# The last chunk's edge sums kept on chip and spread by a 0/1 product

## The chip, the cores and the metric

The kernel is one program on one core of a Trainium2 chip. The core has TensorE (PE; its weight loads are listed as PEld), VectorE (DVE), ScalarE (ACT), GpSimd (POOL) and SyncE (SP), each with its own queue of instructions, which it takes strictly in order. DMAs are issued by the SP, ACT and POOL queues. The metric is the device time of one execution in microseconds, as a median of several runs; lower is better.

## The reference

One graph layer over 10,000 nodes of 512 features, 160,000 edges sorted by `dst`, all in float32:

```python
xn = _layernorm(x, axis=-1)
x = x + gnn(xn) + attention(xn)        # gnn: relu(segment_sum(h[src'] * w, dst') + bias), h = xn @ W
x = x + experts(_layernorm(x, axis=-1))
```

`gnn` is called with the arrays `src` and `dst`. For each edge it takes a row of normalised features, times the edge's weight, summed into the node of the other end; since the product with `W` is linear, the kernel sums rows first and multiplies by `W` (`wg`) afterwards. `attention` is linear attention with softmax over the features of the queries and over the tokens of the keys, followed by a layer norm without mean shift; `experts` weighs six two-layer networks by a router that sees the mean over all tokens, so it can't be finished before the last row of `x` is known.

## The kernel before

The nodes are cut into 20 chunks (`NCH`): 19 of 512 rows (128 partitions x `SUB` = 4) and a last one of 272 (68 partitions x 4). There are three stages.

**Keys and queries** (up to 1350 us) makes keys, queries and the attention's matrix `G`. From its third chunk on, edges run beside it.

**Rows** (to 2143 us) goes through the chunks. `attention(c)` multiplies the stored queries of chunk c with `mix` (`po`, L1048) and normalises; it runs `MIXED` = 3 chunks ahead. The loop of L1063 then takes the chunk's edge sums `at` (fetched by `gathered`), transposes them into `aT` (`nodes_rows`, L1071, ACT copies them out of PSUM), multiplies by `wg` (`pg`, L1087), adds bias, relu and attention on DVE, stores the row to `x1_d` (L1091) and takes statistics.

**Experts** (from 2143 us) goes through the chunks again: rows come back from `x1_d` (`rows_in`, four DMAs), ACT normalises them (`normalising`, L351), DVE transposes them and makes sums of halves (`turned_in`, `xs`), and PE multiplies by weights and sums of weights (`w_sum`, made by `sums_of_weights` once `w1` is loaded).

**The edges.** The 1250 tiles of 128 edges are cut into 866 windows of at most two tiles; four windows make one of 217 groups (`NQ`). For a group, POOL gathers the source rows by an indirect DMA a tile (`msg`, L583), DVE makes the selecting matrix `sel` (L589, L591), PE sums them into a 128 x 512 PSUM tile `pm` (L601: 32 rows a window), ACT copies it to `part` (L604) and stores it in `part_d` (L605). There are 24 `msg` buffers, three `part` buffers and two for `pm`. `work(us)` (L698) sets the pace: every product that is put out lets `done[1]` grow by an assumed cost, 0.83 us a matmul, and as many groups as fit are put out with it. `far_enough(c)` (L996) forces all groups out that chunk c's sums need, before they are fetched.

Two neighbouring windows can share nodes, so each window's first four rows hold what belongs to the window before. `carry(w, end)` (L672) is a DMA on POOL's queue that adds such rows in DRAM, over the ranges between the entries of `CARRIES`; the fetch `gathered(c)` (L1013) is an indirect DMA on POOL's queue that reads by the rows of `row_of`, which `find_rows` works out.

The end of the rows stage: in the turn of chunk 17 (`NCH - 3`), `all_edges_in` (L1005) puts out all groups still missing (211 to 216), the last carry and the fetches of chunks 18 and 19, frees the edge buffers (`edge_ctx.close()`) and asks for the expert weights, which take their place. Only then come chunk 19's attention, chunk 17's transposes and its product. In the turn of chunk 18 the first expert rows are asked for (L1117).

**Order.** Inside `manual_schedule` PE runs its instructions in the order in which the program writes them. On the other engines, and on the DMA queues, a planner orders the instructions by its own cost model and by the order of writing, and adds the semaphores. `behind(inst, other)` makes one instruction follow another on its engine. A buffer of a pool is reused once its readers and DMAs are done, a freed pool's memory likewise.

If the input doesn't fit the windows' assumptions, which DVE counts into `n_odd`, `general_path` does all edges again by scatter; on the given input it isn't taken.

Of the kernel before, what the change touches and what calls it, by code (L numbers as in the profile page):

```python
# [9 lines left out]
F32 = mybir.dt.float32  # L10
# [7 lines left out]
P = 128  # L18
SQ = 32
# [18 lines left out]
MIXED = 3  # L38

AT_HAND = [(5, 320), (7, 384), (8, 424), (9, 472), (10, 520), (11, 560), (12, 604), (13, 640), (14, 680), (15, 716), (16, 752),  # L40
           (17, 788), (18, 820)]
# [11 lines left out]
]  # L53


@with_exitstack
def gps_layer_kernel(
# [91 lines left out]
    ZERO_ROW = NQ * P  # L149
# [74 lines left out]
    def sums_of(o, a11, a12, a21, a22):  # L224

        nc.vector.tensor_tensor(o[0], a21, a22, ALU.add)  # L226
        nc.vector.tensor_tensor(o[2], a11, a21, ALU.subtract)  # L227
        nc.vector.tensor_tensor(o[1], o[0], a11, ALU.subtract)  # L228
        nc.vector.tensor_tensor(o[3], a12, o[1], ALU.subtract)
# [149 lines left out]
    def sums_of_weights():  # L379
        w1_sb, w1_sum = held_w["w1"], held_w["w1_sum"]  # L380
        p_half, q_half = slice(0, PAIRS * P), slice(PAIRS * P, 2 * PAIRS * P)
        sums_of([w1_sum[:, i] for i in range(4)], w1_sb[:, :KH, p_half], w1_sb[:, KH:, p_half],
                w1_sb[:, :KH, q_half], w1_sb[:, KH:, q_half])
# [4 lines left out]
    with ExitStack() as ph:  # L388
# [54 lines left out]
        n_odd = ep.tile([1, 1], I32, name="n_odd")  # L443

# [79 lines left out]
        def window_at(node, more):  # L524
            tile_no = NET * (node / N) ** 0.5 + more
            return min(max(int(tile_no / 2 if tile_no < 2 * PAIRED else tile_no - PAIRED), 0), NW)

        def span(c):
            return window_at(chunks[c][0], -SPARE), window_at(chunks[c][0] + SUB * chunks[c][1], SPARE)

        def spans_hold():
            for c, (b, r) in enumerate(chunks):
                for i, w, op, edge in ((0, span(c)[0], ALU.is_le, b), (1, span(c)[1], ALU.is_ge, b + SUB * r)):
                    at = 3 + len(AT_HAND) + 2 * c + i
                    nc.vector.tensor_scalar(count[:, at : at + 1], bases[:, w : w + 1], float(edge // SUB), None, op0=op)
# [59 lines left out]
        def edges_summed(i, batch, m, sel):  # L595

            pm = psum_e.tile([P, D], F32, name="pm")
            for j in range(batch):
                for h in range(GROUP):
                    k = h * batch + j  # L600
                    nc.tensor.matmul(pm[h * WIN : (h + 1) * WIN, :], sel[:, k, :], m[k] if k < len(m) else m[0],  # L601
                                     start=j == 0, stop=j == batch - 1, skip_group_check=True)
            part = pools["w"].tile([P, D], F32, name="part")
            nc.scalar.copy(part, pm)  # L604
            nc.scalar.dma_start(part_d[i * P : (i + 1) * P, :], part)  # L605
# [39 lines left out]

        def next_nodes():
            pn = psum.tile([P, 1], F32, name="pnext", tag="ps")
            nc.tensor.transpose(pn[:CHAINED], bases[0:1, 1 : CHAINED + 1], ident[0:1, 0:1])
            nc.vector.tensor_copy(nexts[:CHAINED], pn[:CHAINED])
# [26 lines left out]
        carried = []  # L676
        for i in range(PARTS):
            carried.append((past(CHAINED // GROUP, i * LAG), partial(carry_loads, i)))
            carried.append((past(CHAINED // GROUP, (i + 1) * LAG), partial(carry_chained, i)))
# [5 lines left out]
        ahead = [AHEAD]  # L685
        EARLY_TOTAL = PRODUCT * KB * ROWS_IN * 3 * KB
# [11 lines left out]
        def work(us):  # L698

            done[1] += us  # L700
            if not pools:

                normal_rows(int(done[1] / EARLY_TOTAL * (NCH + 1)) + 4 - len(normal))
                return
            edges_to(groups_of(int(done[1] / pace[0])))
# [14 lines left out]
        def all_edges(fp):  # L720
# [12 lines left out]
            nc.vector.tensor_copy(row_of, four)  # L733
            dst_sb = fp.tile([P, NET], I32, name="dst_far")
# [121 lines left out]
        for c, (_, r) in enumerate(chunks):  # L856
# [67 lines left out]
            if c == CHECKED:  # L924
                next_nodes()
                oddities()
            if c >= CHECKED:
                find_rows(c, added)
                if c < 2 * CHECKED:
                    find_rows(c - CHECKED, added)  # L930
# [65 lines left out]
        def far_enough(c):  # L996

            for n, w in AT_HAND:
                if c < n:
                    edges_to(min(NQ, past(w // GROUP, lag_of(w) + LEAD) + 1))  # L1000
                    return w * WIN
            assert not pools
            return ZERO_ROW + P

        def all_edges_in():  # L1005
            edges_to(NQ)
            carry(CARRIES[-1], NW - 1)
            assert not carried
            pools.clear()
            edge_ctx.close()  # L1010
            experts_weights()

        def gathered(c):  # L1013
            r = chunks[c][1]
            n_rows = far_enough(c)
            at = io.tile([P, SUB, D], F32, name="at", tag="at" if c < NCH - 1 else "qT")
            nc.gpsimd.indirect_dma_start(
                out=at[:r].rearrange("p s d -> p (s d)"), out_offset=None, in_=by_four[: n_rows // SUB, :],
                in_offset=bass.IndirectOffsetOnAxis(ap=row_of[:r, c : c + 1], axis=0))
            return at  # L1020
# [17 lines left out]
        def attention(c, beside):  # L1038
# [3 lines left out]
            qT, xt = held.pop("last") if c == NCH - 1 else (queries_in(c), rows_again(c))  # L1042
# [20 lines left out]
        for c, (_, r) in enumerate(chunks):  # L1063
            ot, at = mixed.pop(0), ats.pop(0)
            aT = io.tile([P, KB, SUB * P], F32, name="aT", bufs=1)

            if c == NCH - 3:
                all_edges_in()
                ats += [gathered(c + 1), gathered(c + 2)]
# [4 lines left out]
            if c + MIXED < NCH - 1:  # L1074
                mixed.append(attention(c + MIXED, nodes_rows))
            elif c == NCH - 3:
                mixed.append(attention(NCH - 1, nodes_rows))
            else:
                nodes_rows()
            if c < NCH - 3:  # L1080
                ats.append(gathered(c + 1))
            if c == NCH - 4:
                held["last"] = queries_in(NCH - 1), rows_again(NCH - 1)

            for s in range(SUB):
# [3 lines left out]
                nc.vector.tensor_tensor(po[:r, :], po[:r, :], bias_b[:r], ALU.add)  # L1089
# [17 lines left out]
            if c == NCH - 3:  # L1107
                sums_of_weights()
            if c == NCH - 2:
                io_f["in"] = ctx.enter_context(tc.tile_pool(name="f_in", bufs=1, reuse_waits="tile"))  # L1110

                io_f["squares"] = io_f["in"].tile([P, P // SQ, P], F32, name="squares")
                for b in range(P // SQ):
                    nc.vector.tensor_copy(
                        io_f["squares"][:, b].rearrange("k (g t) -> k g t", t=SQ),
                        ident[:, None, b * SQ : (b + 1) * SQ].to_broadcast([P, P // SQ, SQ]))
                xn = rows_in(0)  # L1117
                st = small.tile([P, P // SQ, 1, SUB, 2], F32, name="st_sq", bufs=1)
                stats_of_squares(st, 0)
                for step in normalising(0, xn, st[:, :, 0]):  # L1120
                    step()
                turn = turned_in(0, rows_turned(0, xn))
# [350 lines left out]
```

## Time and profile before

| | |
|---|---|
| median of 3 runs | 3536.73 us (3527.2 to 3548.53) |
| profiled execution | 3518.48 us, its span 3516.7 us |
| PE busy | 3256.7 us (93%), 12819 matmul instructions |
| DVE, ACT, POOL busy | 1766.5, 831.1, 1311.2 us |
| mean granted clock of TensorE | 0.961 |
| edge gathers (`msg`) | 1250 issues, 984 ns each on POOL |
| last edge gather issued / last group's matmuls | 2059.89 us / 2067.9 us |
| first expert matmul | 2142.57 us |

The profile is of one execution. Times in it count from the first instruction. A line of the timeline gives start, length, engine, source line, operation, what it writes and reads, and in brackets how long the engine was idle before and what ended that wait ("issue": nothing that the profile shows). A float32 matmul appears as two records; 0.43 us apart for 512 columns. A table of windows gives the busy time of each engine in a stretch, the granted clock, and the share of time that the DMA engines were busy.

### The profile page before, as it was taken

How to read it: one execution, taken by the hardware profiler on the slowest of the kernel's cores; microseconds unless marked ns; L12 is line 12 of the kernel's file. 1: busy time of each engine (PE TensorE's matmuls, PEld its weight loads, DVE VectorE, ACT ScalarE, POOL GpSimd, SP SyncE). 2: the span in 40 equal slices, each digit the busy share in tenths (PEclk: the TensorE clock that was granted, in tenths of full speed). 3: DMA queues.
4: the chain of work that ended last, by engine and by line, in shares of the span. 5: the costliest groups of instructions: out<-in, count | busy, mean ns of one | idle time of the engine just before them, and what ended most of it. 6: DMA issues, size and time to landing. Idle time of an engine off the chain costs nothing. (4 is left out here: it accounts for less than half of the span.)

```text
span 3516.7 us, 36142 instructions
## 1 busy us (share of the span) xinstructions
PE 3256.7 (93%) x12819; PEld 1916.0 (54%) x12819; DVE 1766.5 (50%) x3902; ACT 831.1 (24%) x1674; POOL 1311.2 (37%) x1421
## 2 busy tenths in 40 slices
PE   6899998988999989898998988999999999999998
PEld 3433333333333333333333335888888888888886
DVE  6644445444444425564565557445445544544542
ACT  5321212121112112121222113222222222222221
POOL 3466666665666656676676630000000000000000
PEclk8999999999999979899999988999999999999999
DMA  9677777776777878898998882221212212122111
GB/s 392 235 217 249 227 247 248 254 223 208 227 223 243 247 275 318 313 332 293 318 336 301 294 268 61 60 75 58 60 57 76 60 49 84 49 60 73 60 37 38
DMA packets 216735, 654.39 MB, mean 186 GB/s; under 512 B 34425, under 2 KB 74361, under 8 KB 188831
## 3 DMA queue, kind: packets, MB, share of 16 engines
q0 software_dynamic: 104096, 354.29, 32.0%
q1 hardware_dynamic: 69992, 175.33, 15.2%
q10 hardware_dynamic: 42452, 122.31, 9.0%
q8 instruction: 105, 1.72, 0.2%
q14 instruction: 90, 0.74, 0.1%
HBM read 491.21 MB, written 166.63 MB: 187 GB/s over the span
## 5 line engine op out<-in xcount | busy, mean ns | idle before, releaser
L583 POOL DMA_INDIRECT msg<-xn_d,src_sb x1250 | 1229.9, 984 | 634.4 <-issue 287.2
L601 PE MATMUL pm<-msg,sel 128*32 128x512 f32 x2504 | 351.7, 617 | 54.5 <-issue 44.5
L911 PE MATMUL pc<-xn,ek 128*128 128x512 f32 (+1 forms) x640 | 306.5, 624 | 20.5 <-issue 15.0
L209 PE MATMUL po<-G,qT 128*128 128x512 f32 (+1 forms) x640 | 302.0, 613 | 13.0 <-issue 12.2
L209 PE MATMUL pg<-wq,aT 128*128 128x512 f32 (+1 forms) x640 | 301.3, 617 | 10.2 <-issue 9.0
L604 ACT COPY part<-pm 128x512 f32<-128x512 f32 x217 | 127.1, 586 | 733.9 <-PE pm L601 276.0
L601 PEld LDWEIGHTS pm<-msg,sel 128*32 128x32 f32 x2504 | 66.1, 110 | 302.7 <-issue 266.2
L209 PEld LDWEIGHTS pg<-wq,aT 128*128 128x128 f32 (+1 forms) x640 | 117.7, 192 | 195.7 <-issue 184.7
L911 PEld LDWEIGHTS pc<-xn,ek 128*128 128x128 f32 (+1 forms) x640 | 122.7, 199 | 177.4 <-issue 164.7
L209 PEld LDWEIGHTS po<-G,qT 128*128 128x128 f32 (+1 forms) x640 | 117.4, 191 | 185.6 <-issue 181.4
L243 PE MATMUL px<-xnT,w_sb 128*128 128x256 f32 (+1 forms) x800 | 204.6, 379 | 6.8 <-DVE u L1290 6.8
L243 PE MATMUL p<-kq_sum,xs_b 128*128 128x512 f32 (+1 forms) x432 | 201.4, 600 | 3.2 <-issue 2.4
L166 DVE BATCH_NORM_STATS2 st<-ot 128x6 f32<-128x512 f32 (+1 forms) x160 | 110.3, 689 | 178.5 <-issue 119.2
L243 PE MATMUL px<-w_sb,hh 128*128 128x256 f32 (+1 forms) x800 | 185.7, 379 | 0.0
L243 PE MATMUL py<-xs,w_sum 128*128 128x256 f32 (+1 forms) x800 | 185.3, 374 | 0.0
L243 PE MATMUL p<-wk,xnT 128*128 128x512 f32 (+1 forms) x288 | 148.1, 637 | 34.9 <-issue 26.7
L243 PE MATMUL py<-w_sum,hh 128*128 128x256 f32 (+1 forms) x800 | 179.2, 379 | 0.0
L589 DVE TENSOR_TENSOR sel<-iota_w,place 128x128 f32<-128x128 f32 (+2 forms) x217 | 74.5, 344 | 206.1 <-remote 86.2
L243 PEld LDWEIGHTS px<-xnT,w_sb 128*128 128x128 f32 x800 | 150.7, 192 | 29.9 <-DVE u L1290 10.0
L243 PEld LDWEIGHTS py<-w_sum,hh 128*128 128x128 f32 (+1 forms) x800 | 150.0, 188 | 22.7
L243 PEld LDWEIGHTS px<-w_sb,hh 128*128 128x128 f32 (+1 forms) x800 | 150.0, 188 | 22.7
L243 PEld LDWEIGHTS py<-xs,w_sum 128*128 128x128 f32 x800 | 149.8, 190 | 19.9
(298 smaller groups left out, 4577.4 us busy)
## 6 DMA issues: line engine op xcount, KB each, us to landing
part_d<-part ACTq DMA_DIRECT2D x217, 256.0 KB
msg<-xn_d,src_sb POOLq DMA_INDIRECT x1250
xn<-in_x SPq DMA_DIRECT2D x19, 1024.0 KB
xn_d<-xn ACTq DMA_DIRECT2D x19, 1024.0 KB
qT_d<-qT ACTq DMA_DIRECT2D x19, 1024.0 KB
qT<-qT_d SPq DMA_DIRECT2D x19, 1024.0 KB
xt<-in_x SPq DMA_DIRECT2D x19, 1024.0 KB
x_d<-ot SPq DMA_DIRECT2D x19, 1024.0 KB
```

The lines of the kernel that those rows point to most:

```text
L166: nc.vector.bn_stats(st[:r, s, :], t[:r, s, :])
L209: nc.tensor.matmul(po[:r, :], t[:, kb, s * r : (s + 1) * r], w[:, kb, :], start=kb == 0, stop=kb == KB - 1)
L243: nc.tensor.matmul(o, lhs[j], rhs[j], start=start and j == 0, stop=stop and j == n - 1, skip_group_check=True)
L583: nc.gpsimd.indirect_dma_start(out=m[k], out_offset=None, in_=xn_d, in_offset=bass.IndirectOffsetOnAxis(ap=src_sb[:, t0 + k : t0 + k + 1], ...
L589: nc.vector.tensor_tensor(sel[:, :n], iota_w[:, None, :].to_broadcast([P, n, WIN]), place[:, t0 : t0 + n, None].to_broadcast([P, n, WIN]), ...
L601: nc.tensor.matmul(pm[h * WIN : (h + 1) * WIN, :], sel[:, k, :], m[k] if k < len(m) else m[0], start=j == 0, stop=j == batch - 1, skip_gro ...
L604: nc.scalar.copy(part, pm)
L911: nc.tensor.matmul(pc, ek[:r, s, cb * P : (cb + 1) * P], xn[:r, s, :], start=s == 0, stop=s == SUB - 1)
```

## The change

The edge sums of the last six groups (211 to 216, `ON_CHIP` = 211) stay in SBUF, in two tiles of three groups (`parts`, in the buffers of the queries `qT`). Only groups up to 213 (`STORED` = 214) are also written to DRAM. A carry is made up to window 853 instead of 820 for chunk 18; there is none behind it.

The last chunk's sums are made on PE. `nodes_on_chip` (in chunk 5 of the keys stage) notes for each row of a kept group which node it stands for. `numbered` compares these with the numbers of the last chunk's 272 nodes: a 0/1 matrix of 128 x 272 for each of the six groups. `last_sums` multiplies the kept sums with it, 128 features at a time, giving the transposed sums that the product with `wg` wants, the carry's addition included. It is called twice: with the first four groups (`FIRST_SUMS`) after chunk 17's product, written to `aT_last` by ACT copies, and with the other two in the turn of chunk 19, together with `at` (by a product with the identity), added on DVE. On the given input `at` is now a fetch of 68 rows that are all the row of zeros (`row_of` = `ZERO_ROW`), so that the general path can still use it.

The order changes too. Chunk 19's attention is written in the turn of chunk 16. Chunk 17's transposes and product come before `all_edges_in`, with the groups held back at 215 (`limit`) until then. The first expert rows are asked for ahead of the expert weights. The sums of weights move behind the first expert inputs, and chunk 19's additions are ordered behind them.

```diff
+FIRST_SUMS = 4
 AT_HAND = [(5, 320), ..., (16, 752),
-           (17, 788), (18, 820)]
+           (17, 788), (18, 820), (19, 853)]
...
-    ZERO_ROW = NQ * P
+    ON_CHIP = window_at(N, NET, chunks[-1][0], -3) // GROUP
+    STORED = -(-CARRIES[-1] // GROUP)
+    ZERO_ROW = STORED * P
...
-            part = pools["w"].tile([P, D], F32, name="part")
+            if i < ON_CHIP:
+                part = pools["w"].tile([P, D], F32, name="part")
+            else:
+                if (i - ON_CHIP) % 3 == 0:
+                    parts.append(io.tile([P, 3, D], F32, name="parts", tag="qT"))
+                part = parts[-1][:, (i - ON_CHIP) % 3, :]
             nc.scalar.copy(part, pm)
-            nc.scalar.dma_start(part_d[i * P : (i + 1) * P, :], part)
+            if i < STORED:
+                nc.scalar.dma_start(part_d[i * P : (i + 1) * P, :], part)
...
+        def nodes_on_chip():
+            nc.vector.memset(node_of, FAR)
+            for h in range(GROUP):
+                n = -(-(NW - ON_CHIP * GROUP - h) // GROUP)
+                for q, next_one in ((WIN, 0), (SUB, 1)):
+                    rows = slice(h * WIN, h * WIN + q)
+                    at = node_of[rows, :n]
+                    w = ON_CHIP * GROUP + h + next_one
+                    nc.vector.tensor_scalar(at, bases[rows, w : w + GROUP * (n - 1) + 1 : GROUP], float(SUB), spare[rows],
+                                            op0=ALU.mult, op1=ALU.add)
+                    nc.vector.tensor_scalar(at, at, float(-N - h * WIN - (0 if next_one else SUB)), None, op0=ALU.add)
+            nc.vector.tensor_scalar(row_of[:, NCH - 1 :], four[:, NCH - 1 :], 0.0, float(ZERO_ROW // SUB),
+                                    op0=ALU.mult, op1=ALU.add)
...
-            edges_to(groups_of(int(done[1] / pace[0])))
+            edges_to(min(groups_of(int(done[1] / pace[0])), limit[0]))
...
             if c == CHECKED:
+                nodes_on_chip()
                 next_nodes()
                 oddities()
             if c >= CHECKED:
-                find_rows(c, added)
+                if c < NCH - 1:
+                    find_rows(c, added)
...
         def all_edges_in():
             edges_to(NQ)
-            carry(CARRIES[-1], NW - 1)
+            ats.append(gathered(NCH - 2))
+            ats.append(gathered(NCH - 1))
             assert not carried
             pools.clear()
             edge_ctx.close()
+            io_f["in"] = ctx.enter_context(tc.tile_pool(name="f_in", bufs=1, reuse_waits="tile"))
+            rows_first = rows_in(0)
             experts_weights()
+            io_f["squares"] = ...
+            return rows_first
+
+        def numbered():
+            b, r = chunks[-1]
+            mine = io.tile([P, NQ - ON_CHIP + 1, SUB, r], F32, name="mine", tag="xt", bufs=1)
+            number = mine[:, NQ - ON_CHIP]
+            nc.gpsimd.iota(number, pattern=[[1, SUB], [SUB, r]], base=b, channel_multiplier=0,
+                           allow_small_or_imprecise_dtypes=True)
+            for g in range(NQ - ON_CHIP):
+                nc.vector.tensor_scalar(mine[:, g], number, node_of[:, g : g + 1], None, op0=ALU.is_equal)
+            return mine
+
+        def last_sums(o, mine, groups, at):
+            n = SUB * chunks[-1][1]
+            for kb in range(KB):
+                kbs = slice(kb * P, (kb + 1) * P)
+                pt = psum.tile([P, SUB * P], F32, name="pt", tag="ps")[:, :n]
+                for g in groups:
+                    nc.tensor.matmul(pt, parts[g // 3][:, g % 3, kbs], mine[:, g].rearrange("p s n -> p (s n)"),
+                                     start=g == groups[0], stop=at is None and g == groups[-1], skip_group_check=True)
+                if at is None:
+                    nc.scalar.copy(o[:, kb, :n], pt)
+                    continue
+                r = chunks[-1][1]
+                for s in range(SUB):
+                    nc.tensor.matmul(pt[:, s * r : (s + 1) * r], at[:r, s, kbs], ident[:r, :r],
+                                     start=False, stop=s == SUB - 1, skip_group_check=True)
+                nc.vector.tensor_tensor(o[:, kb, :n], o[:, kb, :n], pt, ALU.add)
...
-            aT = io.tile([P, KB, SUB * P], F32, name="aT", bufs=1)
-
-            if c == NCH - 3:
-                all_edges_in()
-                ats += [gathered(c + 1), gathered(c + 2)]
+            aT = io.tile([P, KB, SUB * P], F32, name="aT", bufs=1) if c < NCH - 1 else aT_last
...
-            if c + MIXED < NCH - 1:
+            if c + MIXED < NCH:
                 mixed.append(attention(c + MIXED, nodes_rows))
-            elif c == NCH - 3:
-                mixed.append(attention(NCH - 1, nodes_rows))
+            elif c < NCH - 1:
+                nodes_rows()
             else:
-                nodes_rows()
+                last_sums(aT, mine, range(FIRST_SUMS, NQ - ON_CHIP), at)
...
+            if c == NCH - 3:
+                limit[0] = ON_CHIP + FIRST_SUMS
             for s in range(SUB):
...
-                nc.vector.tensor_tensor(po[:r, :], po[:r, :], bias_b[:r], ALU.add)
+                added = nc.vector.tensor_tensor(po[:r, :], po[:r, :], bias_b[:r], ALU.add)
+                if c == NCH - 1:
+                    behind(added, weights_summed)
...
             if c == NCH - 3:
-                sums_of_weights()
+                mine = numbered()
+                aT_last = io.tile([P, KB, SUB * P], F32, name="aT_last", tag="ot", bufs=MIXED + 2)
+                edges_to(limit[0])
+                last_sums(aT_last, mine, range(FIRST_SUMS), None)
+                rows_first = all_edges_in()
             if c == NCH - 2:
-                io_f["in"] = ...
-                xn = rows_in(0)
                 st = small.tile([P, P // SQ, 1, SUB, 2], F32, name="st_sq", bufs=1)
                 stats_of_squares(st, 0)
-                for step in normalising(0, xn, st[:, :, 0]):
+                for step in normalising(0, rows_first, st[:, :, 0]):
                     step()
-                turn = turned_in(0, rows_turned(0, xn))
+                turn = turned_in(0, rows_turned(0, rows_first))
+                weights_summed = sums_of_weights()
```

## The prediction

> **What bounds the kernel now.** I read the table of windows first, because the edit touches one place: the end of the edge sums and the start of the expert stage. Columns: window, its length, busy us (instructions) of PE, PEld, DVE, ACT, POOL, then granted clock, DMA share, GB/s.
>
> ```profile
> 1450.00:2020.00 570.00, 531.61 (x1830) 199.72 (x1828) 323.82 (x840) 116.52 (x225) 390.59 (x392) 0.96 0.90 314
> 2020.00:2070.00 50.00, 34.03 (x141) 11.55 (x141) 25.66 (x70) 9.09 (x19) 27.73 (x29) 0.80 0.86 289
> 2070.00:2143.00 73.00, 59.32 (x182) 26.22 (x181) 55.52 (x112) 15.43 (x38) 6.33 (x45) 0.92 0.68 188
> ...
> 2197.00:3517.00 1320.00, 1301.49 (x5940) 1109.36 (x5939) 626.66 (x1256) 335.17 (x812) 0.00 (x0) 0.99 0.20 60
> ```
>
> PE is the bound before 2020 and after 2197. Between them, in 123 us, it idles 30 us and runs at a lowered clock. So whatever moves the start of the experts (2142.57) moves the end one for one. PE's timeline shows where the idle time lies (start, length, instruction group, idle time before it):
>
> ```profile
> 2029.07 1.49 PE L601 MATMUL pm<-msg,sel 128*32 128x512 f32 x8 [2.47 <-ACT part L604]
> 2033.89 1.93 PE L601 MATMUL pm<-msg,sel 128*32 128x512 f32 x8 [3.32 <-issue]
> ...
> 2057.26 1.93 PE L601 MATMUL pm<-msg,sel 128*32 128x512 f32 x8 [3.65 <-issue]
> 2064.32 4.15 PE L601 MATMUL pm<-msg,sel 128*32 128x512 f32 x24 [5.12 <-ACT part L604]
> 2068.40 10.52 PE L209 MATMUL po<-G,qT 128*68 128x512 f32 x24
> ...
> 2083.93 13.90 PE L209 MATMUL pg<-wq,aT 128*128 128x512 f32 x32
> 2097.66 1.91 PE L201 MATMUL pt<-ident,at 128*128 128x128 f32 x16
> ...
> 2142.57 2.04 PE L243 MATMUL px<-xs,w_sum 128*128 128x256 f32 x4 [13.68 <-DVE xs L235]
> ```
>
> PE stands in the last edge groups with three pieces of ready work behind them: chunk 19's attention (2068.40), chunk 17's node product (2083.93) and chunk 18's. Then it waits 13.68 us for the experts' first input. Why, ACT's timeline tells: the normalising of expert chunk 0 stands behind chunk 19's root.
>
> ```profile
> 2131.51 0.20 ACT L174 ACTIVATE root<-ve 68x4 f32<-68x4 f32 x1 [11.06 <-DVE ve L169]
> 2131.84 6.26 ACT L351 ACTIVATE xn<-xn,st_sq 128x128 f32<-128x128 f32 x16
> ```
>
> POOL's timeline gives the last edge gather, the last carry and the fetches of chunks 18 and 19:
>
> ```profile
> 2059.89 0.95 POOL L583 DMA_INDIRECT msg<-xn_d,src_sb  x1 [0.30 <-issue]
> 2075.94 0.96 POOL L673 DMA_DIRECT2D part_d<-part_d  x1 [15.10 <-DMA b_sb<-in_b_a]
> 2082.06 1.04 POOL L1017 DMA_INDIRECT at<-part_d,row_of  x1 [5.16 <-DMA part_d<-part_d]
> 2083.39 1.12 POOL L1017 DMA_INDIRECT at<-part_d,row_of  x1 [0.30 <-issue]
> ```
>
> **The change, part by part.**
>
> *Order on PE (gain).* From group 206 (2021.79) to the transposes of chunk 18 (2097.66) PE takes 75.9 us. Its work there, by undisturbed pitches: 11 groups at 1.00, two transposes 1.89 + 1.75, two node products at 13.73, one attention at 13.78: 55.9. So 20.0 us are idle or half-clock time. The edit puts chunk 19's attention before group 211 and chunk 17's product among groups 211 to 214. By the same pitches, with the pacing rule at 3.32/0.96 tiles a product (attention: groups 207 to 209, forced group 210; product 16: groups 211, 212; product 17: 213, 214): product 16 ends at 2058.1, group 213 at 2064.3, product 17 at 2075.6. The gathers don't move: POOL issues one each 1.25 us up to 2059.89, and the buffers of groups 207 to 210 come free by 2042, before POOL needs them. So data are there some 15 us before PE asks, and the 20.0 us go. What would bring them back: gathers later by over 15 us.
>
> *Chunk 19's sums on PE (cost).* Part one: 4 blocks x 4 groups = 16 products of 272 columns; a 256-column product takes 0.43 us in the expert rows (four records from 2149.34 to 2150.20), so 0.46 each, 7.4 us. Part two: 8 such, 3.7; 16 small products with the identity instead of 16 transposes (1.03 us), between 1.03 and twice that, as they may take two passes: +0 to +1; I take 0, the rows being of the same shape. All on PE's path: +11.1, of which 7.4 before chunk 18.
>
> *Experts' first input (gain).* Its rows are fetched one chunk earlier and all four loads stand before the weights, not two of them behind chunk 18's store. Chunk 19's adds come after the weights' sums, so the normalising no longer has chunk 19's root ahead of it. The 13.68 go, and 1.45 more: the first pair of experts, at half clock, took 7.63 against 6.18 for the second. What covers it: DVE work after product 18 is chunk 18's tail 6.8, the four additions 1.7, transposing 2.3, input sums 2.6, weight sums 5.8 = 19.2 us; PE has sums 3.7, statistics 0.8, transposes 1.0 and product 19 13.9 = 19.4. A tie, so any DVE delay shows.
>
> *New wait 1: chunk 18's rows.* Before, 13.78 + 1.75 + 13.73 us of PE work covered carry and fetch. Now the chain starts at group 213: copy 0.6, issue 0.4, landing of the store 3.4 (2070.61 to 2074.02), carry 7.4 (2033.00 to 2040.36), fetch 0.3 + 5.8 (2041.10 to 2046.90) = 17.9. PE has 3.43 + 1 + 6.87 of product 17 and group 214, part one 7.4 and groups 215, 216 at 2.0 = 20.7. Slack 2.8, so 0; with the longest rows (store 5.7, fetch 12.4 beside the weights' load, 2082.06 to 2094.5) it is 26.8, a wait of 6. I take 1. Queued behind the carry on POOL are only the two fetches; the ones who wait are PE's transposes of chunk 18 and all behind them.
>
> By the Trainium skill ("DMA: Bandwidth & Descriptors", Anatomy of one DMA) a transfer costs about 2 us plus its bytes at 436 GB/s. By that the store, the carry and the fetch would be some 10 us together (an estimate) and the slack about 10; the trace's 5.85 to 7.4 us for a carry of a quarter megabyte speaks against it, and the sum keeps the rows.
>
> *New wait 2: product 19 behind DVE.* Its input is now finished by DVE additions, not ACT copies. Part two ends at 2105.9 on PE; DVE is in chunk 18's tail until 2107.2, then 1.7 for the four. I take 3 us. If the planner places these additions behind input and weight sums, PE waits until 2119.6, or 13.7. Below zero it can't be.
>
> *New wait 3: the marks* (one iota, six comparisons of 272 columns, 0.42 each by the 256-column DVE rows, 2.6). Their buffer is free once chunk 19's attention is done (about 2046), 30 us before use: 0, at most 3 if they queue behind chunk 17's tail. The iota sits in POOL's queue before the carry; a 32-column one took 0.157, so under 1.4 and in a queue that idles then.
>
> *Loads.* w1 and w2 can start only when the edge buffers are free: 2085, not 2070.6. The first weight sum ran at 2094.58, 24 us after the first issue; so w1 is there by 2109, before DVE reaches the sums (2114). w2 is asked for only 40 us later. Covered; if not, DVE's tie breaks and each us counts. ACT stores three parts less (0.33 each, off the path).
>
> *Early in the kernel.* 18 small DVE instructions at chunk 5 (0.16 to 0.2 each, 3.5 us) against one row search less there; DVE is busy 427 of 950 us in that stage. 0, with a reordered plan worth up to 5 us either way.
>
> **Sum.** -20.0 + 7.4 = -12.6 up to chunk 18; +3.7 and -13.7 - 1.45 after it: -24.1. New waits 1 + 3: -20. The profiled execution took 3518.48 (span 3516.7), so 3498; the median shown, 3536.73, is 18 above that execution, so for the median 3517.
>
> **The clock.** The windows show that waits cost more than their length:
>
> ```profile
> 2030.00:2039.50 9.50, 6.18 (x17) 1.89 (x14) 3.42 (x11) 1.66 (x3) 6.43 (x7) 0.50 0.94 289
> ...
> 2057.00:2067.00 10.00, 4.62 (x24) 0.80 (x24) 2.46 (x10) 1.97 (x5) 2.93 (x4) 0.50 0.77 261
> ```
>
> After idle time of 2.5 to 5 us the grant was 0.50 for some 10 us: up to 5 us of work lost. So a new wait over about 3 us costs up to 5 more. The skill ("TensorE: Matmul & The Clock Gate", What's actually happening) lets the clock return after about 3.4 us of sustained work. By it the extra would be about 2 us (an estimate); the two windows say more.
>
> **Rivals.**
>
> 1. *DVE holds product 19.* For: a tie of 19.2 against 19.4 us, and in the profile of before DVE mixes weight sums among chunk 18's adds (2111.26 to 2116.7). Against: their data come late. Price 13.7 instead of 3: -9, or 3528, less 0 to 5 for the clock.
>
> 2. *Carry or fetch of chunk 18 behind the weights (other side).* For: the last carry of before stood 15.10 us behind a small bias load on another queue. Against: now it is issued 15 us before any weight can load. If POOL's order or a shared completion count ties it to w1, its rows come 24 (load) + 7.4 + 6.1 = 37.5 us after 2085: -24 + 37.5 + 3 + 5 (clock) = +21, 3558. It takes 24 us of wait to lose the gain and 42 in all to be slower by 0.5%.
>
> 3. *The idle time was supply after all.* If gathers slip along with PE (buffers are freed later by one attention, 14 us), the first 20 us stay and 11.1 are added: +11.1 - 15.1 + 3 = -1, 3536. Against: the buffers' times above.
>
> **How the numbers follow.** Forecast 0.50, rival 1 0.22, rival 2 0.12, rival 3 or a worse plan early on 0.16. About 0.5%, 17.7 us, is what a measurement can tell from no change. Of the forecast's 0.50 some 0.4 lie beyond it, and 0.06 more come from fewer waits than taken; rival 2 gives 0.12 slower, a worse plan 0.05. So faster 0.46, same 0.37, slower 0.17. The likeliest case alone spans 3505 (no new wait, early plan 8 better) to 3523 (chunk 18's rows 6 late); with rivals 1 and 3 and a spread of 10 us among the runs, 3502 to 3545.
>
> **What would show it.** Right: PE without a gap over 2 us from 2022 to 2086, clock 1.00; the experts' first product near 2123; ACT's normalising before chunk 19's root; no 13.68. Wrong: idle time on PE before the transposes of chunk 18 (POOL's carry or fetch as releaser), before product 19 (DVE), or before the first expert product with the input or weight sums named.

## The result and the profile after

The changed kernel takes 3536.91 us (median of 21 runs, 3521.92 to 3552.44), the kernel before 3536.73 us in the same runs: a ratio of 1.0002, 95% interval 0.9989 to 1.0015. Two later comparisons gave 0.9999 (0.9980 to 1.0018) and 0.9988 (0.9969 to 1.0007). The forecast of 3517 did not come; at most 0.3% can be hidden in the last interval.

The executions differ by some 20 us in the stages before the change (chunk 15's product with `wg` starts at 2002.7 us in the profile before, at 2028.9 in the one after), so I compare the tail, by PE's timeline, in two stretches. **A** runs from the first product of chunk 15 with `wg` to the transposes of chunk 18, **B** from there to the third expert pair. Before: A 95.0, B 64.9 us. After: A 91.8, B 63.7. From the third pair to the end it is 1354.1 and 1353.7. So in this pair of executions the tail won 4.3 us, where 20 were forecast (24 less 4 for waits).

The windows of the profile after (columns as in the table shown of before):

```profile
2020.00:2070.00 50.00, 49.17 (x189) 18.02 (x186) 34.80 (x96) 15.35 (x30) 35.55 (x33) 1.00 0.90 295
2070.00:2143.00 73.00, 66.39 (x244) 33.91 (x243) 39.99 (x94) 14.27 (x34) 18.58 (x59) 0.93 0.69 184
2143.00:2197.00 54.00, 49.12 (x194) 32.30 (x194) 38.29 (x74) 17.02 (x43) 0.00 (x0) 0.94 0.46 140
```

Where PE idled in 2020 to 2070 before (34.03 us busy at 0.80), it is busy all the time at full clock. The idle time is now in the two windows behind it. PE's timeline of the kernel after shows the places:

```profile
2083.45 1.04 PE L209 MATMUL pt<-ident,at 128*128 128x128 f32 x8
2086.99 0.66 PE L209 MATMUL pt<-ident,at 128*128 128x128 f32 x4 [2.50 <-issue]
2089.66 1.11 PE L209 MATMUL pt<-ident,at 128*128 128x128 f32 x4 [2.01 <-DVE ot L1156]
2092.29 6.64 PE L217 MATMUL pg<-wq,aT 128*128 128x512 f32 x8 [1.52 <-DVE ot L1156]
...
2111.45 7.50 PE L1070 MATMUL pt<-mine,parts 128*128 128x272 f32 x32
...
2123.27 14.00 PE L217 MATMUL pg<-wq,aT 128*128 128x512 f32 x32 [0.57 <-ACT aT L211]
2137.11 0.95 PE L345 MATMUL pst<-stats,squares 128*128 128x8 f32 x8
2137.92 1.16 PE L1070 MATMUL pt<-mine,parts 128*128 128x272 f32 x4
2138.92 1.01 PE L1077 MATMUL pt<-ident,at 68*128 68x68 f32 x8
...
2145.20 13.90 PE L217 MATMUL pg<-wq,aT_last 128*68 128x512 f32 x32
2158.93 1.03 PE L251 MATMUL px<-xs,w_sum 128*128 128x256 f32 x4
...
2169.16 2.07 PE L251 MATMUL px<-xnT,w_sb 128*128 128x256 f32 x4 [4.88 <-DVE u L1353]
2171.03 3.02 PE L345 MATMUL pst<-stats,squares 128*128 128x80 f32 x16
2173.88 1.08 PE L251 MATMUL px<-xs,w_sum 128*128 128x256 f32 x4
```

Three things are to be seen. Chunk 17's transposes take 8.84 us (2083.45 to 2092.29) instead of 1.75, and the eight records of its product behind them 6.64 instead of 3.6: the granted clock of 2092 to 2096 is 0.50. Part two of chunk 19's sums takes 7.3 us (2137.92 to 2145.20). The first expert pair waits 4.88 us for DVE in front of its last product, which then takes 2.07 us instead of 1.03 (the granted clock of 2169 to 2172 is 0.50 again). Before the experts' first product (2158.93), where 13.68 us were idle, nothing is.

DVE's timeline of the same execution tells why PE waited at both places:

```profile
2072.13 0.69 DVE L1153 TENSOR_TENSOR pg<-pg,bias_b 128x512 f32<-128x512 f32 x1
2085.97 0.36 DVE L1061 TENSOR_SCALAR mine<-mine,node_of 128x272 f32<-128x272 f32 x1 [13.16 <-issue]
2086.25 0.68 DVE L1156 SCALAR_TENSOR_TENSOR ot<-pg,ot 128x512 f32<-128x512 f32 x1
...
2157.82 1.29 DVE L1153 TENSOR_TENSOR pg<-pg,bias_b 68x512 f32<-68x512 f32 x2
...
2166.67 1.91 DVE L192 TENSOR_SCALAR wq<-ot,stats 68x512 f32<-68x512 f32 x4
2168.62 0.16 DVE L1164 SCALAR_TENSOR_TENSOR stats<-stats 68x4 f32<-68x4 f32 x1
2168.70 0.41 DVE L1353 TENSOR_TENSOR u<-u,px 128x256 f32<-128x256 f32 x1
```

In the first place DVE stands 13.16 us in front of the first comparison for `mine`, between the two additions of chunk 16. So chunk 16's product isn't taken out of PSUM, and PE finds no buffer for chunk 17. The profile calls this wait "issue", but the iota that the comparison reads ended just then; it is on POOL, behind the last edge gather:

```profile
2084.58 0.95 POOL L590 DMA_INDIRECT msg<-xn_d,src_sb  x1 [0.30 <-issue]
2085.55 0.39 POOL L1058 IOTA mine<- 128x272 f32 x1
2104.56 0.97 POOL L701 DMA_DIRECT2D part_d<-part_d  x1 [18.63 <-issue]
```

In the second place DVE does all that chunk 19 leaves it, 10.9 us of additions, statistics and normalising (2157.82 to 2168.70), before the first pair's addition `u`.

### The profile page after: what moved, and what is told of

It reads as the page before. It is cut to its first block, busy times and chain, and to the rows that moved or that the text cites. A ratio compares the mean times of both kernels' runs of the same rounds, so it can differ in the third digit from the quotient of the medians.

```text
span 3538.2 us, 36288 instructions
## 1 busy us (share of the span) xinstructions
PE 3284.4 (93%) x12883; PEld 1931.6 (55%) x12883; DVE 1767.0 (50%) x3926; ACT 829.9 (23%) x1674; POOL 1317.9 (37%) x1422
## 5 line engine op out<-in xcount | busy, mean ns | idle before, releaser
L608 PE MATMUL pm<-msg,sel 128*32 128x512 f32 x2504 | 360.9, 610 | 45.9 <-issue 39.3
L942 PE MATMUL pc<-xn,ek 128*128 128x512 f32 (+1 forms) x640 | 308.8, 630 | 19.2 <-issue 10.9
L217 PE MATMUL pg<-wq,aT 128*128 128x512 f32 x608 | 290.6, 621 | 25.3 <-issue 22.2
L217 PE MATMUL po<-G,qT 128*128 128x512 f32 (+1 forms) x640 | 294.1, 603 | 4.4 <-issue 4.2
L217 PEld LDWEIGHTS pg<-wq,aT 128*128 128x128 f32 x608 | 112.4, 195 | 204.0 <-issue 188.8
```

Of the source, the lines that this page charges most:

```text
L217: nc.tensor.matmul(po[:r, :], t[:, kb, s * r : (s + 1) * r], w[:, kb, :], start=kb == 0, stop=kb == KB - 1)
L942: nc.tensor.matmul(pc, ek[:r, s, cb * P : (cb + 1) * P], xn[:r, s, :], start=s == 0, stop=s == SUB - 1)
```

## The experiments

The runs fell into two groups. In one the kernel before takes 3515 to 3538 us, in the other 3301 to 3303, since the stages ahead of the tail are shorter (attention begins at 1112 us instead of 1286; from the third pair to the end it is 1352 instead of 1354). What sets the groups apart is not shown; the chip numbered 5 stands in runs of both. Times and stretches are compared within one group only.

| kernel | before, us | this, us | ratio, 95% | A | B |
|---|---|---|---|---|---|
| before, profile of the start | | | | 95.0 | 64.9 |
| after | 3536.73 | 3536.91 | 1.0002 (0.9989 to 1.0015) | 91.8 | 63.7 |
| after_timed | 3515.09 | 3513.78 | 0.9999 (0.9980 to 1.0018) | 91.5 | 63.7 |
| after_third | 3537.57 | 3534.00 | 0.9988 (0.9969 to 1.0007) | 96.8 | 63.4 |
| p1_order | 3515.09 | 3530.44 | 1.0049 (1.0028 to 1.0071) | 105.1 | 69.2 |
| p2_rows_first | 3515.09 | 3508.26 | 0.9977 (0.9957 to 0.9998) | 98.1 | 59.4 |
| e3b_third | 3537.57 | 3523.24 | 0.9961 (0.9942 to 0.9979) | 88.0 | 56.6 |
| *the quicker group:* before_again | 3300.66 | 3291.77, one execution | | 104.8 | 64.8 |
| after_again | 3300.66 | 3296.43, one execution | | 103.3 | 63.4 |
| e1_iota | 3300.66 | 3284.50 | 0.9953 (0.9938 to 0.9967) | 90.8 | 63.9 |
| e1_second | 3303.18 | 3288.12 | 0.9955 (0.9942 to 0.9969) | 90.7 | 64.1 |
| e2_pool_sums | 3300.66 | 3292.94 | 0.9975 (0.9963 to 0.9986) | 92.6 | 68.8 |
| e3b_late_rows | 3303.18 | 3278.03 | 0.9923 (0.9910 to 0.9937) | 86.3 | 56.6 |

**Both kernels once more.**

> The kernel before, once more, to see how far one execution's stages differ from another's. Read: the start of chunk 15's node product (2002.7 us in the first profile of before, 2028.9 in that of after), and the tail from there to the third expert pair's first product (159.9 us before, 155.5 after). Theory (the 26 us by which the profile of after is late at chunk 15 are the spread between executions): the start lies anywhere between 1995 and 2035 us here, the tail stays within 3 us of 159.9. Rival (the change makes the early stages slower): the start lies within 5 us of 2003.

> The changed kernel once more. Theory (spread between executions): the start of chunk 15's node product differs from 2028.9 us by up to 30, the tail stays within 3 us of 155.5, with the same two waits on PE, before the transposes of chunk 17 and in the first expert pair. Rival (early stages slower by the 15 small DVE instructions near 107 us or by what they shift): start within 5 us of 2029, some 20 above the other run of before.

These two executions fell into the quicker group, so neither expectation came as it was written: chunk 15's product starts at 1768.7 and 1774.3 us, and the tails are 169.6 and 166.7. The changed kernel's is 2.9 us shorter. Both waits are there again, and here the profile names the releaser of the first. DVE's timeline of after_again:

```profile
1825.05 0.69 DVE L1153 TENSOR_TENSOR pg<-pg,bias_b 128x512 f32<-128x512 f32 x1
1843.24 0.36 DVE L1061 TENSOR_SCALAR mine<-mine,node_of 128x272 f32<-128x272 f32 x1 [17.50 <-POOL mine L1058]
```

**The iota out of POOL's queue (e1_iota, e1_second).** The numbers of the last chunk's nodes are made once, at the start of the kernel, and kept:

```diff
+    number = const.tile([P, SUB, chunks[-1][1]], F32, name="number")
+    nc.gpsimd.iota(number, ...)
...
-            number = mine[:, NQ - ON_CHIP]
-            nc.gpsimd.iota(number, ...)
```

> The changed kernel with the numbers of the last chunk's nodes made once at the start, not by an iota behind the edge gathers on POOL. Theory: DVE's first comparison no longer waits, so chunk 16's sums leave PSUM in time and PE runs through the transposes of chunk 17 (8.8 us there in the profile of after, 1.75 undisturbed, and 3.1 us of half clock behind it): tail 155.5 - 10 = 145.5 us, total 10 us under the changed kernel, ratio to before 0.997. Rival (the transposes wait for chunk 17's fetched rows or for ACT's copies as well): tail 152 to 156, ratio 1.000.

> The changed kernel with the node numbers made early, a second time, beside the kernel that also moves chunk 19's statistics. Theory (the stall before chunk 17's product is the iota in POOL's queue, 10 us of the tail on any chip): ratio 0.995 to 0.997, tail 145 to 156 us, no stall of PE at chunk 17's transposes. Rival (the first gain of 16 us was more than the tail shows and came from that chip): ratio 0.998 or more.

Ratios of 0.9953 and 0.9955, tails of 154.8 and 154.7 us: 12 less than after_again (10 were expected). PE's timeline of e1_iota at chunk 17's transposes and at the first pair:

```profile
1836.00 1.91 PE L212 MATMUL pt<-ident,at 128*128 128x128 f32 x16
1837.74 3.60 PE L220 MATMUL pg<-wq,aT 128*128 128x512 f32 x8
...
1911.92 2.07 PE L254 MATMUL px<-xnT,w_sb 128*128 128x256 f32 x4 [5.23 <-DVE u L1353]
```

The stall and its half clock are gone (1.74 us instead of 12.7 in after_again), the wait of the first pair is not. So the first wait is shown. With it mended, the gain over the kernel before is about the same in time and in the tail: 16 and 15 us of time, 15 of tail against before_again, 12 of them this wait.

**Weight sums on POOL (e2_pool_sums).** On top of e1_iota, the four sums of expert weights go from DVE to POOL, to free 6 us of DVE; the order that put chunk 19's additions behind them goes with it:

```diff
-        nc.vector.tensor_tensor(o[0], a21, a22, ALU.add)
+        eng.tensor_tensor(o[0], a21, a22, ALU.add)      # eng = nc.gpsimd for w_sum; the other three likewise
...
-                if c == NCH - 1:
-                    behind(added, weights_summed)
```

> As the one with the early iota, and the four sums of weights are made on POOL instead of DVE, without the ordering of chunk 19's additions behind them. Theory (DVE's 6 us of weight sums and then chunk 19's tail delay the first expert pair): the wait of 4.9 us and 2 us of half clock there go too, tail 145.5 - 7 = 138.5 us, ratio to before 0.994 to 0.995. Rival (POOL needs much longer than DVE's 1.49 us a sum, so the first product waits for the weight sums): POOL at 3 us a sum would end them near the end of chunk 19's product, tail 139 to 143; at 6 us a sum the first product waits some 10 us, tail 150.

This theory fell: the tail became 6.7 us longer than in e1_iota (4.9 of it in B; the rest lies ahead of the sums, in A), and the wait for `u` grew from 5.23 to 7.00. DVE's timeline of e2_pool_sums, then POOL's:

```profile
1888.93 2.65 DVE L189 TENSOR_TENSOR near<-root 128x4 f32<-128x4 f32 x1
...
1898.87 3.37 DVE L245 TENSOR_TENSOR xs<-xnT 128x512 f32<-128x512 f32 x1
1902.16 3.37 DVE L246 TENSOR_TENSOR xs<-xnT 128x512 f32<-128x512 f32 x1
1905.45 0.68 DVE L247 TENSOR_TENSOR xs<-xnT,xs 128x512 f32<-128x512 f32 x1
```

```profile
1888.67 2.89 POOL L239 TENSOR_TENSOR w_sum<-w_sb 128x1280 f32<-128x1280 f32 x1 [28.36 <-DMA w_sb<-in_w]
...
1898.47 3.21 POOL L240 TENSOR_TENSOR w_sum<-w_sum,w_sb 128x1280 f32<-128x1280 f32 x1
1901.76 3.22 POOL L241 TENSOR_TENSOR w_sum<-w_sb,w_sum 128x1280 f32<-128x1280 f32 x1
```

A DVE product of 4 columns that takes 0.16 elsewhere takes 2.65 and ends with POOL's first sum; the input sums take 3.37 instead of 0.68, as long as POOL's sums beside them. The Trainium skill ("SBUF — State Buffer", SBUF: two separate sides) has an exclusive lock there: of a DVE operation with two SBUF inputs and a GpSimd operation that reads SBUF, the one that starts first holds the shared ports for its whole length. The rows agree: DVE's transposing of `xn`, with one input, kept its 2.30 us.

**The order alone (p1_order).** The kernel before with chunk 19's attention in the turn of chunk 16 and chunk 17's product ahead of `all_edges_in`; chunk 19's sums still go through memory.

```diff
-            if c == NCH - 3:
-                all_edges_in()
-                ats += [gathered(c + 1), gathered(c + 2)]
...
-            if c + MIXED < NCH - 1:
+            if c + MIXED < NCH:
...
             if c == NCH - 3:
+                all_edges_in()
+                ats += [gathered(c + 1), gathered(c + 2)]
                 sums_of_weights()
```

> The kernel before with the new order alone: chunk 19's attention in the turn of chunk 16's transposes, chunk 17's node product ahead of the last groups; chunk 19's sums still go through memory, with a last carry. Theory (the order pays only together with the sums on the chip, which cover the chain that ends in chunk 18's rows): the 20 us of idle and half-clock time before chunk 17's product go, but PE then waits 16 to 18 us at chunk 18's transposes for carry and fetch, and up to 5 us of lowered clock follow; tail 165 to 175 us (169.6 in the kernel before), ratio 0.998 to 1.002. Rival (the order alone brings the gain): tail 150, ratio 0.994.

Slower by 0.49%, more than expected: the tail takes 174.2 us, 14 more than in the profile before, which is of the same group. PE's timeline of p1_order, then POOL's:

```profile
2082.85 1.07 PE L601 MATMUL pm<-msg,sel 128*32 128x512 f32 x8
2108.75 3.67 PE L201 MATMUL pt<-ident,at 128*128 128x128 f32 x16 [24.83 <-DMA at<-part_d,row_of]
...
2158.04 2.07 PE L243 MATMUL px<-xs,w_sum 128*128 128x256 f32 x4 [15.90 <-DVE xs L235]
```

```profile
2091.83 0.96 POOL L673 DMA_DIRECT2D part_d<-part_d  x1 [30.75 <-DMA b_sb<-in_b_a]
2098.10 1.03 POOL L1017 DMA_INDIRECT at<-part_d,row_of  x1 [5.32 <-DMA part_d<-part_d]
```

Copy, store, carry and fetch of chunk 18 take 24.8 us when nothing covers them: the fetch, from 2098.10, runs beside the weights' load and lands some 10 us later. (The profile has the carry released by a small bias load on ACT's queue, as in the kernel before; whether this load or the store of the sums came last isn't shown.) Without that wait and the 2 us of half clock behind it, A would be 78 us, 17 less than before; the wait takes all of this back and A ends 10 us longer. So the on-chip sums aren't a saving themselves; they are 7.5 us of PE work that stands where PE would wait, with a carry that can be asked for earlier. How much is due to each of the two wasn't tried apart.

**The experts' side alone (p2_rows_first).** The kernel before with the first expert rows asked for before the weights, the weights' sums behind the first inputs, chunk 19's additions behind those.

```diff
         def all_edges_in():
...
+            rows_first = rows_in(0)
             experts_weights()
...
-            if c == NCH - 3:
-                sums_of_weights()
...
+                if c == NCH - 1:
+                    behind(added, weights_summed)
```

> The kernel before with the experts' side of the change alone: the first chunk's rows asked for before the weights, the weights' sums behind the first inputs, chunk 19's additions behind the weights' sums. Theory: the wait of 13.7 us before the first expert product goes, as in the changed kernel, and a wait of about 5 us of the first pair for DVE (whose queue holds chunk 19's whole tail ahead of that pair's first addition) comes with some 2 us of lowered clock: tail 7 us shorter than before (162 to 164), ratio 0.998. Rival (the wait of 13.7 us hides other work that then ends last): tail 169, ratio 1.000.

The ratio is 0.9977 and B is 5.5 us shorter (the whole tail 2.4): the ratio that was expected, but with another wait. PE's timeline of p2_rows_first, then ACT's:

```profile
2126.71 16.23 PE L209 MATMUL pg<-wq,aT 128*68 128x512 f32 x32 [6.14 <-ACT aT L203]
...
2149.15 1.13 PE L243 MATMUL px<-xnT,w_sb 128*128 128x256 f32 x4 [1.03 <-DVE u L1291]
```

```profile
2122.45 3.94 ACT L351 ACTIVATE xn<-xn,st_sq 128x128 f32<-128x128 f32 x10
2126.30 1.20 ACT L203 COPY aT<-pt 128x272 f32<-128x272 f32 x4
```

The 13.7 us are gone, but the normalising of expert chunk 0 now stands on ACT ahead of the copies of chunk 19's transposes: 6.14 us of wait and 2.3 of half clock. In the changed kernel these copies were ACT's in part one, long before, and part two is added on DVE. Only so are both gone.

**Chunk 19's tail behind the first pair (e3_late_rows, e3b_late_rows, e3b_third).** On top of e1_iota, chunk 19's rows are kept in the buffer of `wg` and their statistics and normalising move behind the first pair's additions on DVE; the reciprocal root goes to POOL (two small instructions, 0.24 and 1.04 us), so that ACT needs no other table in between (a table load takes it 1.28 us in the kernel after).

```diff
-            row_stats(ot, r, mv)
-            if c == NCH - 1:
-                normalize(wg, ot, r, mv)
+            if c == NCH - 1:
+                continue
+            row_stats(ot, r, mv)
...
+        row_stats(wg, r, mv, on_pool=True, after=first_v[0])    # each bn_stats behind the first pair's last addition
+        normalize(wg, wg, r, mv)
...
-        router = [all_stats, ...]
+        router = [lambda: (last_rows(), all_stats()), ...]
```

> The changed kernel with the node numbers made early (as in the kernel that does that alone: ratio 0.9953) and chunk 19's statistics and normalising moved behind the first expert pair's additions on DVE (its reciprocal root on POOL, three small instructions), so that this pair's first addition stands behind chunk 19's additions alone. Theory (the 5 us wait of the first pair is DVE's order): that wait goes, with some 2 us of lowered clock; tail 147 to 150 us against 154.8; ratio about 0.993. Rival (DVE has no slack here, the wait only moves to the second pair or to the mean's products): tail 153 to 156, ratio 0.995.

In this first form (3519.10 us beside 3515.09, ratio 1.0010, 0.9987 to 1.0033) the additions of one quarter of chunk 19 overwrite `wg` while the next quarters' products still have to read it. These products multiply other numbers, so the result is wrong, and they wait for DVE (10.85 us before the second quarter, 0.65 in the third). It says nothing on the theory. In the next form all four products come first:

```diff
+                if c == NCH - 1:
+                    last_po.append(po)
+                    continue
                 nc.vector.scalar_tensor_tensor(ot[:r, s, :], po[:r, :], 0.0, ot[:r, s, :], ...)
+            for s, po in enumerate(last_po):
+                nc.vector.scalar_tensor_tensor(wg[:r, s, :], po[:r, :], 0.0, ot[:r, s, :], ...)
```

> The same, and chunk 19's four second additions made after all four of its products, into the buffer of the weights that these products read; its statistics and normalising behind the first expert pair's additions on DVE, its reciprocal root on POOL. Theory (the 5 us wait of the first pair is DVE's order): the wait and some 2 us of lowered clock go; from the first expert product to the third pair 20 us instead of 25.6; ratio 0.002 below that of the kernel beside it. Rival (DVE has no slack, the wait moves to the second pair or to the mean's products): 24 to 26 us, the same ratio.

The ratio is 0.9923, 0.0032 below e1_second beside it; from the first expert product to the third pair it takes 18.4 us instead of 25.9. PE's timeline of e3b_late_rows, then DVE's:

```profile
1896.54 1.03 PE L256 MATMUL px<-xs,w_sum 128*128 128x256 f32 x4
...
1901.72 1.03 PE L256 MATMUL px<-xnT,w_sb 128*128 128x256 f32 x4
1902.58 1.90 PE L350 MATMUL pst<-stats,squares 128*128 128x80 f32 x16
1904.32 1.08 PE L256 MATMUL px<-xs,w_sum 128*128 128x256 f32 x4
```

```profile
1898.17 2.47 DVE L1164 SCALAR_TENSOR_TENSOR wq<-pg,ot 68x512 f32<-68x512 f32 x4
1900.56 0.41 DVE L1371 TENSOR_TENSOR u<-u,px 128x256 f32<-128x256 f32 x1
...
1902.93 1.28 DVE L177 BATCH_NORM_STATS2 st<-wq 68x6 f32<-68x512 f32 x2
```

`u` is made before PE asks for it, and the first pair takes 7.78 us (1896.54 to 1904.32) instead of 14.95 in the kernel after. DVE did have room, right behind. The same kernel beside the changed one in the slower group:

> The changed kernel as it is, timed on the same chip as the kernels beside it. Theory (three costs of the tail eat a gain of 24 us that is really there): the tail, from chunk 15's node product to the third expert pair, is 3 to 4 us shorter than in the kernel before; the ratio lies between 0.998 and 1.001. Rival (the earlier stages became slower by some 4 us, since chunk 15's node product started at 1774 and not at 1769 in the one look): the ratio is 1.000 to 1.002 and chunk 15's product starts after 1772 again, while the two kernels beside it that change only the tail of the kernel before start it at 1769.

> The changed kernel once more, on one chip with the kernel that mends both of its waits. Its tail 155 us where the keys and rows take long, 167 where they are short (on such a chip the stall before chunk 17's product was longer); ratio 0.998 to 1.001. Were the ratio over 1.002, something before the tail would have become slower too.

> Both waits mended. Theory (PE's own work sets the tail then, and it is the same on each chip): tail 141 to 146 us, ratio 0.992 to 0.995 (17 us off 160 is 0.5% where the kernel before takes 3515; 27 us off 170 is 0.8% where it takes 3300). Rival (the gain belongs to chips with short early stages): ratio over 0.997.

The changed kernel keeps its tie. The tail of after_third is 160.2 us, not the expected 155: there PE also waits twice in chunk 15's product, 3.5 us in all, with half clock behind it. So the tails of the changed kernel run from 155.1 to 160.2, beside the one profile of before in this group with 159.9, and the 4.3 us of the first pair are within this spread. With both waits mended the ratio is 0.9961 (0.9942 to 0.9979), less of a gain than the 0.992 to 0.995 expected, and the tail 144.6: this version beats the kernel before in both groups, and the changed kernel beside it by 11 us. Its A of 88.0 begins at half clock, behind a wait of 3.13 us, which costs 2.8 of it.

One open point was whether something ahead of the tail had become slower too, since chunk 15's product started later in all profiles of the changed kernel's family in the quicker group (1772 to 1777 us against 1768.7) and in the first pair of profiles. The times show no such loss: e1_iota, e1_second and e3b_late_rows won 16, 15 and 25 us of time (give or take some 5) and 15, 15 and 27 of tail. In the slower group the changed kernel's family started that product anywhere from 1990.1 (after_timed) to 2034.3 (e3b_third); p1_order and p2_rows_first, whose early part is that of the kernel before, at 2003.7 and 2005.0. What makes these starts spread wasn't looked into, and a few us there are not excluded.

## Why the prediction was wrong

The forecast was 20 us less; the tail of the first pair of profiles shows 4.3, the times show none. By its own terms: the gain without waits, 24.1, would have been there. The two waits that the sum took, 1 and 3 us, did not come. Three other terms took the gain back: 10.1 + 2.6 + 7.2 = 19.9, and 24.1 - 19.9 = 4.2. That 3536.91 lies between the 3502 and 3545 of the prediction is luck: that stretch was drawn for its rivals, and none of them happened.

**Right: the order on PE.** Taking from A part one (7.5) and the stall (7.1 + 3.0) leaves 74.2 us, against 95.0 before: 20.8 won, 20 forecast. Where the stall is really gone, in e1_iota, A less part one is 83.3, against 104.8 in before_again: 21.5. p1_order shows that without the on-chip sums and their earlier carry the new order loses.

**Right: part one, 7.5 us (7.4 forecast); chunk 18's rows, no wait** (the 0.57 is ACT's copy). The chain was estimated at 17.9 us and at 26.8 with the longest rows; uncovered, in p1_order (with the carry behind a later group), it took 24.8, so the longest rows were the nearer ones.

**Right: product 19 does not wait, the 13.68 go, the weights are there in time.** Rivals 1 to 3 did not happen, and the likeliest case did not either. (Rival 3, late gathers, is not far off: in the quicker group PE does wait for gathers in A, 4.5 us in two waits in after_again.)

**Wrong: "new wait 3", the marks.** It was set at 0 to 3 us, with the iota "in a queue that idles then". It cost 10.1 (7.1 of stall, 3.0 of half clock). The mistake could be read in the profile of before: the last gather leaves POOL at 2059.89, and the forecast itself had product 16 end at 2058.1, so an iota written behind the gathers would come after the moment at which the comparisons could first run. I asked when the buffer was free and how long the iota takes, not what stands before it on its queue. And the planner put the comparison between two additions that PE waits for, so a wait that would have hurt nobody (part one starts at 2111.45, 25 us after the iota) held back chunk 17.

**Wrong size: part two, 7.3 us instead of 4.7** (3.7 + 1.03). The products with the identity appear as two records each where a transpose has one: 0.85 us a block of eight, 3.4 in all instead of 1.03; the eight real products took 4.0. The bound "twice that" was too low; the shape alone didn't set the price. PE's timeline of the kernel before has the transposes:

```profile
2113.96 1.20 PE L201 MATMUL pt<-ident,at 68*128 68x68 f32 x16
2114.99 13.90 PE L209 MATMUL pg<-wq,aT 128*68 128x512 f32 x32
```

**Wrong: "a tie, so any DVE delay shows", but only up to the first product.** The balance of 19.2 against 19.4 us ended at the first expert product, which indeed did not wait. What DVE still owed chunk 19 then, 10.9 us, was counted nowhere, and it stood ahead of the first pair's `u`. The forecast even took 1.45 us off this pair for its clock. It cost 7.2 (4.9 of wait, 2.3 of half clock). e3b_late_rows shows that this was order, not load.

**The clock.** I took up to 5 us of loss behind a wait, from two windows of the profile before, over the roughly 2 us that follow from the skill's rule of about 3.4 us of sustained work ("TensorE: Matmul & The Clock Gate", What's actually happening). The losses measured were 3.0 and 2.3 us here, 2.3 in p2_rows_first: the rule was nearer. In the two windows PE was busy for 6.18 of 9.50 us and 4.62 of 10.00, so further waits lay inside them, and they were no measure of what one wait costs.

## What to carry to other kernels

When an edit adds an instruction to a queue, ask what is ahead of it there, and which engine will stand in front of its result with what behind it; a small iota behind a stream of gathers cost 10 us of the 24 that this change had to win. Where a balance between two engines is a tie, carry it on past the point at which the first wait was removed, until the debt is paid off. A constant is best made where the queue is empty, and work that nobody waits for is best ordered behind the first thing that somebody does.

## What the runs showed of the hardware

DVE operations on two SBUF operands lasted until POOL's tensor addition beside them ended: 0.16 us became 2.65, 0.68 became 3.37, and with 6 us of work moved to POOL, B became 4.9 us longer. After a wait of 5 us PE ran at half clock for 4 to 5 us of work (the first pair after: 2169.16 to 2173.88). And the same program took 3301 to 3303 us in some runs and 3515 to 3538 in others, with the difference ahead of the experts' stage.
